# Reordering the head and the per-image table chain of a deformable convolution kernel

## The chip, the cores and the metric

The kernel runs on one core of one Trainium2 chip. Its time is the device time of one execution in microseconds (us), and the number quoted is the median of several runs. Engines are called by their names in the profile: PE is TensorE's matrix multiply (PEld its weight load), DVE is VectorE, ACT is ScalarE, POOL is GpSimd and SP is SyncE, which only issues DMAs. A name with a q behind it (SPq, ACTq, POOLq) is the queue of that engine, which issues DMAs in program order and waits for what they need.

## The reference

The input x is 8 images of 128 channels of 64 x 64 pixels, float32. There are two layers, each behind a group normalisation:

```
x = x + relu(batchnorm(deform_conv(groupnorm(x))))
x = x + expert_conv(groupnorm(x)) + shared_conv(groupnorm(x))
```

The change is in the first. Its deformable convolution first computes 27 maps of offsets and masks per image with a 3 x 3 convolution (`om`), and then, for each of 9 taps and each pixel, samples the image at a fractional place:

```
py = off_y + row + ky - 1;  px = off_x + column + kx - 1     # 9 taps
val = bilinear(x, py, px) * sigmoid(mask)
out = sum over channels and taps of val * w
```

The second layer mixes four expert kernels per image and convolves with the mixture.

## The kernel before

`dense()` is the first layer, `layer1()` the second. `general()` is a slow way for offsets of two pixels or more and does not run with these inputs.

**Bands.** An image is cut into 8 bands (`NB`) of 8 rows, and the main loop in `dense()` runs over 64 bands (and one closing turn). A band's bilinear sampling is done by matrix multiplication: for a row of 15 tiles (4 x 4 output pixels each, for two tile rows), the 8 x 8 surrounding pixels, turned by `pixels` (L630, ACT copies them out at L635), are multiplied in `sample` (L672) with weights `s`. `weights` (L656, VectorE) makes these as a product of two tents, `x_wts` and `y_wts`, three steps ahead. Then `conv` (L721) multiplies the samples with the taps' weights, in nine matmuls a band, called parts 0 to 8 below; the band after an image's last has 18.

**Tables.** The tents come from two tables per image in DRAM, `x_table` and `y_table`. `load_x` (L590) reads two rows of 576 KB each per band, three bands ahead, and `load_y` (L575) eight pieces of 90 KB per band, two bands ahead; in the main loop both go through POOL's queue. ACT (L606) and VectorE (L608) finish the x tents in `spread`.

**The table chain.** The tables of an image are made by the generator `tables(b)`, in this order: statistics of the image (L290), group means and deviations (L296 and L306 on PE, L312 on POOL), normalisation in place (L318 on ACT, L319 on VectorE), the offsets' convolution in four blocks (`combine` at L345 on VectorE, `tap` at L362 on PE), collecting in `om` (L385 to L395), a turned copy (L402 or L404/L405), stores to DRAM as `rowwise` (L408) and `colwise` (L412), loads back with rows and columns on partitions into `raw_off` (L435, L437), a nudge for the borders (L474), distances in y and x (L478, L487), the x table's store (L458), the mask (L523), five tents (L501, L505, or L510 to L516) times the mask (L537), and the y table's store (L527).

**The order is written out by hand.** Each `yield` in `tables(b)` gives back control, `pause(n)` gives it back n times, and `yield BLOCK` waits until a part in `BLOCKS`. The main loop takes some three steps (`tick`) at every part, so that the chain of a later image lies between the matmuls of an earlier one. Engines run in program order, so where a step is placed decides what queues behind it. The chain of image b + 2 begins in band 5 of image b, at part 4, and must be done one image later. Images 0 and 1 have a head: image 0's chain runs alone, and then image 1's as far as its group scale, before the first band.

The y table is stored skewed: the tent i of row h goes to row h + i of a table with 4 rows more, and the loads read along that diagonal.

Of the kernel before, what the change touches and what calls it, by code (L numbers as in the profile page):

```python
# [41 lines left out]
T = 4  # L42
# [22 lines left out]
def deform_moe_conv(  # L65
# [83 lines left out]
    def padded(pool, name):  # L149
# [12 lines left out]
        for a, n in (("y", (H + 2 * REACH) * GROW), ("x", NROW * XROW))  # L162
# [15 lines left out]
    def dense():  # L178

        with ExitStack() as st:  # L180
# [95 lines left out]

            def tables(b):

                if b == B:
                    return  # L280
                pad = pads[b % 2]
                stats = small.tile([P, NCH, 6], F32, name="stats")
                part = [
                    pad[:, ROWPAD + 8 * c : ROWPAD + 8 * c + 8].rearrange("p h w -> p (h w)")
                    for c in range(NCH)
                ]
                for c in range(NCH):
                    if c == 6 and b > 1:
                        yield from pause(14 if b > 2 else 24)
                    nc.vector.bn_stats(stats[:, c, :], part[c])  # L290
                    yield from pause(2)
                mv = small.tile([P, 2], F32, name="mv")
                nc.vector.bn_aggr(mv, stats)
# [23 lines left out]
                for c in range(0, NCH, 2):  # L317
                    nc.scalar.activation(part[c], part[c], AF.Identity, bias=shift, scale=scale)  # L318
                    nc.vector.tensor_scalar(  # L319
                        part[c + 1], part[c + 1], scale, shift, ALU.mult, ALU.add  # L320
                    )
                    yield from pause(2)
# [10 lines left out]
                def combine(j):  # L333
# [5 lines left out]
                    for half in range(2):  # L339
                        rows = [  # L340
                            pad[:, ROWPAD - 1 + H // 2 * half + i :][:, 0 : H // 2 : 2]
                            for i in (lo, hi)
                        ]
                        n = H // 4
                        nc.vector.tensor_tensor(  # L345
                            combo_of[j][:, half * n : half * n + n], *rows, op
                        )
                        yield from pause(2)
# [7 lines left out]
                def tap(j, kx):  # L356

                    if kx == 1:
                        pcs[j] = ps_c.tile([P, CH], F32, name="pc", tag="pc")
                    lo, hi = max(0, 1 - kx), min(W, W + 1 - kx)  # L360
# [26 lines left out]
                yield from block(2)  # L387
                m2 = taken(2)
                nc.vector.tensor_tensor(odd, even, m2, ALU.subtract)
                nc.vector.tensor_tensor(even, even, m2, ALU.add)  # L390
                yield from combine(3)
# [7 lines left out]
                if b:  # L399
                    for half in (slice(0, H // 8), slice(H // 8, H // 4)):  # L400
                        yield from pause(2)
                        nc.scalar.copy(turned[:, half], by_rows[:, half])  # L402
                else:
                    nc.scalar.copy(turned[:, 0 : H // 8], by_rows[:, 0 : H // 8])  # L404
                    nc.vector.tensor_copy(turned[:, H // 8 :], by_rows[:, H // 8 :])  # L405
                yield from pause(4)
                for j in range(4):
# [3 lines left out]
                    )  # L411
                    (nc.gpsimd if b or j % 2 == 0 else nc.sync).dma_start(  # L412
                        out=colwise[b][:, :, H // 4 * j : H // 4 * (j + 1)],
                        in_=omc[32 * j + 9 : 32 * j + 18],
                    )
                nc.vector.tensor_reduce(
                    most[:, b : b + 1], omr, AX.X, ALU.max, apply_absolute_value=True
                )
                if b == 0:
                    for g in range(2):  # L420
                        pick(g)
                yield from pause(12)
                by_row = rowwise[b].rearrange("h (t k u) w -> h t k (u w)", t=3, k=3)

                for k in range(3):
# [6 lines left out]
                    for outs, parts, v in places:  # L434
                        nc.sync.dma_start(out=raw_off[parts, v], in_=by_row[outs, 0::2, k])  # L435
                        parts = slice(W + parts.start, W + parts.stop)
                        (nc.gpsimd if b or k == 1 else nc.scalar).dma_start(  # L437
                            out=raw_off[parts, v, 0].rearrange("p (u h) -> p u h", u=3),
                            in_=colwise[b][k::3].rearrange("s w h -> w s h")[outs],
                        )  # L440
                if b == 0:
                    for _ in pixels(0):
                        pass
                yield from pause(26)
# [28 lines left out]
                for i in range(2):  # L473
                    nc.vector.tensor_scalar(  # L474
                        raw_off[:, 2 * i, 0], raw_off[:, 2 * i, 0], nudge[:, i : i + 1],
                        None, ALU.add,
                    )
                nc.vector.tensor_copy(by_y, moved(0, 0, "v", "j", "u"))  # L478
                nc.vector.tensor_copy(by_y[:, :, 0, 0], raw_off[sides[0], :, 0, 2 * W])
                nc.vector.tensor_copy(by_y[:, :, W - 1, 2], raw_off[sides[0], :, 0, W - 1])  # L480
                yield from pause(2)
                for out_, in_ in (
                    (by_x, moved(1, 0, "j", "u", "v")),
                    (by_x[:, 0, 0], raw_off[sides[1], :, 0, 2 * W]),
                    (by_x[:, W - 1, 2], raw_off[sides[1], :, 0, W - 1]),
                ):
                    nc.vector.tensor_scalar(out_, in_, in_tile, None, ALU.add)  # L487
                if b:
                    store_x(0, NROW // 2, nc.sync)
                    store_x(NROW // 2, NROW, nc.sync)  # L490
                else:
                    store_x(0, 2, nc.gpsimd)
                    store_x(2, 6, nc.sync)
                yield from pause(2)
# [921 lines left out]
```

## Time and profile before

| what | value |
|---|---|
| median of 3 runs | 1520.25 us (1520.05 to 1520.77) |
| the profiled execution | 1525.29 us, its span 1523.6 us |
| PE busy | 1362.8 us, 89% |
| DVE, ACT, POOL busy | 975.4, 831.0, 527.4 us |
| mean granted PE clock | 0.96 |
| moved by DMA | 227.34 MB, mean 149 GB/s |

The span is from the first to the last instruction. A line of the timeline has start, duration, engine, source line, operation, tile written and tile read, count, and in brackets the idle time before it and what ended it. Lines of waits have who waited for what: total us, times, and the longest.

### The profile page before, as it was taken

Reading aid. Unit: us, or ns where it says so; the run is one execution under the profiler, and the core shown is the slowest. Engines: PE = TensorE matmul, PEld = TensorE weight load, DVE = VectorE, ACT = ScalarE, POOL = GpSimd, SP = SyncE. Lnnn points to the kernel's source line nnn. Section 1 sums busy time; section 2 is a strip of 40 time slices with the busy share of each in tenths; the row PEclk is TensorE's granted clock in tenths of the full one; section 3 lists DMA queues with packets and bytes.
Section 4 is the critical chain, followed back from the end, with each engine's and each line's share of the span. In section 5 each row is a group of like instructions: output and inputs, shape, how many; then the busy total and the mean of one; then the engine's idle time right before and its main releaser. Section 6 shows DMA issues by size and latency. Waiting matters only on the chain. (4 is left out here: it accounts for less than half of the span.)

```text
span 1523.6 us, 21317 instructions
## 1 busy us (share of the span) xinstructions
PE 1362.8 (89%) x7714; PEld 761.6 (50%) x7714; DVE 975.4 (64%) x1905; ACT 831.0 (55%) x1124; POOL 527.4 (35%) x824
## 2 busy tenths in 40 slices
PE   3159899999999989998999999999993899999998
PEld 1044455555555555655555565566551344444443
DVE  5547565666656656655665665655428888889972
ACT  2245664776686567667657766866634333323320
POOL 2222432543353254334425434543303223332300
PEclk9579999999999999999999999999996899999999
DMA  3555884996787589678858967878707044444111
GB/s 129 133 128 113 185 177 105 175 217 133 138 201 173 123 155 221 126 136 199 170 126 168 214 137 142 183 171 200 165 26 302 30 164 166 166 152 166 51 46 58
DMA packets 113932, 227.34 MB, mean 149 GB/s; under 512 B 62238, under 2 KB 68670, under 8 KB 105625
## 3 DMA queue, kind: packets, MB, share of 16 engines
q0 software_dynamic: 52464, 123.79, 40.3%
q1 hardware_dynamic: 59703, 101.03, 21.2%
q8 instruction: 63, 1.03, 0.3%
q10 hardware_dynamic: 1650, 1.06, 0.2%
q14 instruction: 52, 0.43, 0.1%
HBM read 180.23 MB, written 45.35 MB: 148 GB/s over the span
## 5 line engine op out<-in xcount | busy, mean ns | idle before, releaser
L721 PE MATMUL py<-samples,dw_sb 128*128 128x512 f32 (+3 forms) x1296 | 580.1, 565 | 3.1 <-DVE samples L699 1.8
L575 POOL DMA_DIRECT2D ywts<-taby x496 | 294.1, 608 | 303.7 <-DMA xwts<-tabx 244.1
L672 PE MATMUL pq<-s,xt 64*128 64x144 f32 (+1 forms) x3840 | 279.4, 298 | 27.7 <-DVE s L656 19.6
L721 PEld LDWEIGHTS py<-samples,dw_sb 128*128 128x128 f32 x1296 | 219.3, 191 | 156.6 <-issue 134.5
L682 ACT COPY samples<-pq 128x864 f32<-128x864 f32 (+1 forms) x320 | 281.7, 977 | 26.2 <-PE pq L672 26.0
L672 PEld LDWEIGHTS pq<-s,xt 64*128 64x128 f32 x3840 | 253.8, 188 | 77.3 <-issue 30.0
L656 DVE TENSOR_TENSOR s<-xwts,ywts 128x432 f32<-128x432 f32 (+1 forms) x448 | 199.1, 497 | 134.7 <-DMA ywts<-taby 44.9
L635 ACT COPY xt<-pt 128x512 f32<-128x512 f32 (+1 forms) x256 | 142.2, 556 | 175.1 <-PE pt L630 164.7
L630 PEld LDWEIGHTS pt<-ident,picked 128*128 128x128 f32 x960 | 112.1, 142 | 185.0 <-ACT xt L635 116.1
L630 PE MATMUL pt<-ident,picked 128*128 128x128 f32 x960 | 154.1, 281 | 42.7 <-ACT xt L635 38.0
L608 DVE TENSOR_SCALAR xwts<-xwts 128x1152 f32<-128x1152 f32 (+2 forms) x130 | 97.5, 750 | 140.8 <-ACT xwts L606 140.4
L1328 PE MATMUL pc<-v,u 128*128 128x512 f32 x384 | 172.8, 599 | 9.3 <-DVE u L1276 9.3
L1328 PE MATMUL pc<-v,wmix 128*128 128x512 f32 x384 | 177.1, 606 | 0.0
L606 ACT ACTIVATE xwts<-xwts,place 128x1152 f32<-128x1152 f32 (+2 forms) x130 | 161.0, 1242 | 26.3 <-DMA ywts<-taby 20.3
L590 POOL DMA_DIRECT2D xwts<-tabx x128 | 73.2, 577 | 254.8 <-DVE s L656 242.2
L1306 ACT ACTIVATE t<-pc,bmix 128x512 f32<-128x512 f32 x32 | 22.0, 687 | 182.9 <-PE pc L1328 100.9
L1328 PEld LDWEIGHTS pc<-v,u 128*128 128x128 f32 x384 | 72.4, 190 | 98.3 <-issue 85.1
L1328 PEld LDWEIGHTS pc<-v,wmix 128*128 128x128 f32 x384 | 72.7, 192 | 88.9 <-issue 85.2
L729 ACT ACTIVATE y<-py,db_sb 128x512 f32<-128x512 f32 (+3 forms) x72 | 45.8, 636 | 90.8 <-PE py L721 52.3
L345 DVE TENSOR_TENSOR combo<-pad 128x1024 f32<-128x1024 f32 x64 | 75.2, 1220 | 21.8 <-PE pc L362 15.7
L615 DVE COPY picked<-pad 128x960 f32<-128x960 f32 x128 | 82.3, 683 | 0.0
L1155 POOL TENSOR_TENSOR x<-x,xt 128x512 f32<-128x512 f32 x32 | 45.8, 1464 | 85.7 <-ACT x L1153 85.7
(162 smaller groups left out, 1064.9 us busy)
## 6 DMA issues: line engine op xcount, KB each, us to landing
xwts<-tabx POOLq DMA_DIRECT2D x128, 576.0 KB, 7.8
ywts<-taby POOLq DMA_DIRECT2D x496, 90.0 KB, 8.3
pad<-in_x_dram SPq DMA_DIRECT2D x48, 512.0 KB
out_dram<-yo SPq DMA_DIRECT2D x32, 512.0 KB
yd<-y SPq DMA_DIRECT2D x48, 256.0 KB
pad<-yd SPq DMA_DIRECT2D x16, 512.0 KB
x<-yd SPq DMA_DIRECT2D x16, 512.0 KB
xt<-in_x_dram SPq DMA_DIRECT2D x16, 512.0 KB
```

Source lines behind the costliest of these rows:

```text
L345: nc.vector.tensor_tensor(combo_of[j][:, half * n : half * n + n], *rows, op)
L575: engine.dma_start(out=y_wts[g % 2][at : at + NR * Q, r].rearrange("p a b c -> p (a b c)"), in_=bass.AP(tensor=y_table[b].tensor, offset=y ...
L606: nc.scalar.activation(part, part, AF.Abs, bias=column)
L608: nc.vector.tensor_scalar(part, part, -1.0, 0.0, ALU.add, ALU.min)
L615: nc.vector.tensor_copy(picked[g % 2][:, :, h], bass.AP(tensor=one.tensor, offset=one.offset, ap=[list(one.ap[0]), [T, NCOL], [W, Q], [1, Q]],
L630: nc.tensor.transpose(pt[:, c], picked[g % 2][:, c0 + c].rearrange("p h y x -> p (h y x)"), ident,)
L635: nc.scalar.copy(xts[g][:, c0 : c0 + n], pt[:, 0:n])
L656: nc.vector.tensor_tensor(s[:, :, 3 * at : 3 * (at + k)].rearrange("p m (c x) -> p m c x", x=3), by_x[:, :, c : c + k], by_y[:, :, w : w + ...
L672: nc.tensor.matmul(by_m[:, h, :, at : at + k], lhsT=xts[g][rows, c], rhs=s[rows, :, at : at + k], start=True, stop=True,)
L682: nc.scalar.copy(bass.AP(tensor=one.tensor, offset=one.offset + first, ap=[list(one.ap[0]), [M * PLANE, 2], [PLANE, M], [WB + 1, 3], [1, w ...
L721: nc.tensor.matmul(py, lhsT=dw_sb[:, 3 * (2 - yy) + 2 - xx], rhs=samples[g % 2][:, m : m + 3 * n - 2 : 3, xx, 1 : W + 1], start=(i == 0), ...
L1328: nc.tensor.matmul(pc, lhsT=us[j][:, kx], rhs=vs[g][:, rows, kx : kx + W], start=(kx == 0), stop=(kx == 2),)
```

## The change

- `statistics(b)` becomes a generator of its own. In the main loop, its eight steps are taken one per part in bands 6 and 7 of the image two before; `tables(b)` starts at part 2 of band 7, where it was part 4 of band 5. What is left of the chain before is finished at the start of band 6, where it was part 4 of band 5.
- In the chain, the pause between the stores of `om` and their loads grows from 12 to 16 steps, that between the loads and the nudge from 26 to 34, and those around each tent shrink from 3 and 4 to 2 and 2. All rowwise stores now come before all colwise ones.
- The y table is plain: row h holds its five tents side by side.
- For image 0: normalisation has three parts on ACT and five on VectorE; the negation of the taps' weights (`dw_sb`, L766) goes behind the tables; upper halves of three of the four combinations go to GpSimd; the blocks take PSUM buffers of their own (`ps_q`); colwise loads go to SP and GpSimd, behind the rowwise ones; the y side of the nudge and distances no longer waits for the x side; the first y stores have 16 of the 64 rows, the rest comes last; the pixel copies, statistics of image 1, and the loads of later bands change places.

Cut to its core:

```diff
-        for a, n in (("y", (H + 2 * REACH) * GROW), ("x", NROW * XROW))
+        for a, n in (("y", H * GROW), ("x", NROW * XROW))
...
+            def statistics(b):
+                if b >= B:
+                    return
+                stats = small.tile([P, NCH, 6], F32, name="stats")
+                for c, part in enumerate(chunks(b)):
+                    nc.vector.bn_stats(stats[:, c, :], part)
+                    if c == NCH - 1:
+                        means[b] = small.tile([P, 2], F32, name="mv")
+                        nc.vector.bn_aggr(means[b], stats)
+                    yield
...
-                for c in range(NCH):
-                    if c == 6 and b > 1:
-                        yield from pause(14 if b > 2 else 24)
-                    nc.vector.bn_stats(stats[:, c, :], part[c])
-                    yield from pause(2)
-                mv = small.tile([P, 2], F32, name="mv")
-                nc.vector.bn_aggr(mv, stats)
+                mv = means.pop(b)
                 yield BLOCK
...
+                for c in range(NCH):
+                    if c in (0, 2, 4, 6) and (b or c < 6):
+                        nc.scalar.activation(part[c], part[c], AF.Identity, bias=shift, scale=scale)
+                    else:
+                        nc.vector.tensor_scalar(part[c], part[c], scale, shift, ALU.mult, ALU.add)
+                        yield from pause(2)
...
-                        nc.vector.tensor_tensor(
+                        (nc.vector if b or j == 1 or half == 0 else nc.gpsimd).tensor_tensor(
...
-                    if kx == 1:
+                    if kx == 1 and b:
                         pcs[j] = ps_c.tile([P, CH], F32, name="pc", tag="pc")
+                    elif kx == 1:
+                        pcs[j] = ps_q.tile([P, 2, CH], F32, name="pq")[:, 0]
...
-                yield from pause(12)
+                yield from pause(16)
...
+                        if b:
+                            turned_in(nc.gpsimd, k, outs, parts, v)
+                        else:
+                            by_column.append((k, outs, parts, v))
+                for k, *where in by_column:
+                    turned_in(nc.sync if k == 0 else nc.gpsimd, k, *where)
+                yield from pause(34)
-                if b == 0:
-                    for _ in pixels(0):
-                        pass
-                yield from pause(26)
...
-                            offset=y_table[b].offset + i * GROW + (NR - 1 - i) * YSTEP,
-                            ap=[[GROW, H], [GROW - YSTEP, n], [1, YSTEP]],
+                            offset=y_table[b].offset + rows.start * GROW + i * YSTEP,
+                            ap=[[GROW, rows.stop - rows.start], [1, n * YSTEP]],
...
                         yield from tent(i)
-                        yield from pause(3)
+                        yield from pause(2)
                         masked(i)
-                        yield from pause(4)
+                        yield from pause(2)
...
-                load_x(0, nc.gpsimd)
-                for i, k in ((0, 3), (1, 4), (2, None)):
-                    for _ in tent(i):
-                        pass
-                    masked(i)
-                    store_y(i, 1)
-                    if k:
-                        other_tent(k)
-                        masked(k)
-                        store_y(k, 1)
+                for i in (3, 4):
+                    other_tent(i)
+                nudged(sides[1])
+                distances_x()
+                store_x(0, 2, nc.gpsimd)
+                load_x(0, nc.gpsimd)
+                for i in (0, 1, 2):
+                    for _ in tent(i):
+                        pass
+                soon = slice(0, 4 * T)
+                for i in (3, 0, 4, 1, 2):
+                    masked(i)
+                    store_y(i, 1, soon)
+                for _ in pixels(0):
+                    pass
+                for k in range(2 * T):
+                    load_y(0, k, nc.scalar if k in (1, 4, 7) else nc.sync)
+                for _ in statistics(1):
+                    pass
                 for slots in ((NCOL * T, XROW // XSTEP), (0, 12), (12, 36), (36, NCOL * T)):
                     spread(0, slots)
-                for k in range(2 * T):
-                    load_y(0, k, nc.scalar if k % 2 else nc.sync)
-                for g in (1, 2):
-                    load_x(g, nc.gpsimd)
+                store_x(2, 6, nc.gpsimd)
+                load_x(1, nc.gpsimd)
+                for k in range(2 * T):
+                    load_y(1, k, nc.sync)
+                load_x(2, nc.gpsimd)
                 store_x(6, NROW, nc.gpsimd)
-                for k in range(2 * T):
-                    load_y(1, k, nc.scalar if k < 4 else nc.sync)
+                store_y(0, NR, slice(4 * T, H))
...
+                if j == NB - 2:
+                    for _ in made:
+                        pass
+                    asked, made, means_of = True, iter(()), statistics(b + 2)
...
+                    if odd == 0 and (j == NB - 2 and part < 6 or j == NB - 1 and part < 2):
+                        next(means_of, None)
+                    if odd == 0 and j == NB - 1 and part == 2 and b + 2 < B:
+                        made = tables(b + 2)
+                        next(made)
...
-                        if j == 5:
-                            for _ in made:
-                                pass
-                            asked = False
-                            made = tables(b + 2) if b + 2 < B else iter(())
```

## The prediction

> **What bounds the kernel now.** The sum is made on the profiled execution: span 1523.6 us, 1525.29 us in all. The median of the other runs is 1520.25 us, 5.0 us below; I carry differences over to it unchanged. 0.2% (3.0 us) is about what a measurement of this kernel can tell from no change.
>
> First the page's second part, 40 slices of 38.1 us.
>
> ```profile
> PE   3159899999999989998999999999993899999998
> ...
> PEclk9579999999999999999999999999996899999999
> ```
>
> TensorE is full in the bands; only the first two or three slices (the head) and slice 31 (into the second layer, not touched) are empty. So a shift of the head counts in full, and in the bands only idle TensorE time counts. Next the timeline of the head.
>
> ```profile
> 59.89 6.64 SPq L527 DMA_DIRECT2D taby<-work  x5
> 59.96 2.66 POOL L590 DMA_DIRECT2D xwts<-tabx  x5
> ...
> 79.02 11.63 ACTq L575 DMA_DIRECT2D ywts<-taby  x8
> 79.05 10.20 SPq L575 DMA_DIRECT2D ywts<-taby  x8
> 90.86 1.80 DVE L656 TENSOR_TENSOR s<-xwts,ywts 128x432 f32<-128x432 f32 x4 [12.61 <-DMA ywts<-taby]
> ```
>
> The five y stores are issued by 66.5 and the first y load starts at 79.02: 12.5 us of landing. The loads take 11.8 us more. The stretches (PE, PEld, DVE, ACT, POOL busy, then clock, DMA share, GB/s) say why:
>
> ```profile
> 66.00:72.00 6.00, 0.00 (x0) 0.00 (x0) 2.78 (x7) 2.77 (x4) 0.00 (x0) 0.50 1.02 257
> 72.00:78.00 6.00, 1.08 (x4) 1.00 (x4) 4.68 (x11) 0.00 (x0) 0.00 (x0) 0.50 1.00 258
> 84.00:90.00 6.00, 0.00 (x0) 0.00 (x0) 0.00 (x0) 0.00 (x0) 0.00 (x0) 0.50 0.30 109
> ```
>
> Until 78 the DMA engines are full: six x loads of 576 KB (3.46 MB) and 0.74 MB of y stores. While only y loads run they move 109 GB/s at a share of 0.30. Last, TensorE's waits from 120 to 1125:
>
> ```profile
> PE pt L630 <- ACT xt L635: 25.8, 8, 6.7
> PE pq L672 <- ACT samples L682: 7.8, 8, 1.3
> ```
>
> By image, the first is 6.7, 1.0 (1.3 with one of 0.3), 3.0, 5.9, 4.7, 3.4, 0.7 for images 1 to 7. Image 4's, in the timelines of VectorE and ScalarE:
>
> ```profile
> 559.37 1.79 DVE L656 TENSOR_TENSOR s<-xwts,ywts 128x432 f32<-128x432 f32 x4 [9.12 <-DMA combo<-colwise]
> 561.08 0.54 DVE L474 TENSOR_SCALAR combo<-combo,nudge 128x192 f32<-128x192 f32 x2
> ...
> 561.65 1.20 ACT L523 ACTIVATE combo<-combo 64x576 f32<-64x576 f32 x3 [5.55 <-DVE combo L474]
> ...
> 564.19 0.56 ACT L635 COPY xt<-pt 128x512 f32<-128x512 f32 x1
> ```
>
> VectorE waits for late y loads, the nudge (L474) queues behind, ScalarE waits at the mask (L523), and the copy that TensorE needs is behind the mask.
>
> **Head, up to the offsets.** The ScalarE negation of dw (L766, ended 19.4) goes behind; its normalisation can start at 14.0 like VectorE's: 3 x 0.73 = 2.2 there, 5 x 0.48 = 2.4 on VectorE, done 16.4. The first combination started at 20.89: -4.4. The next three blocks' upper halves go to GpSimd. No 1024-element one is in the trace; 128x528 took 1.10, 128x512 mean 1.46 and at most 2.36 (L1155), so 2.1 to 4.7, and I take 2.9, twice the mean beside a busy VectorE. The Trainium skill (GPSIMD Engine Reference, Key points) speaks against this: GpSimd shares its SBUF interfaces with VectorE instructions that have two SBUF inputs, as the halves beside it have; the 2.36 may be that, and at 4.7 the next sum loses 2 us. With own PSUM buffers, blocks 2, 0 and 3 follow block 1 (17.7 + 5.05 = 22.8) at 2.8 to 2.9 each: 31.3, last subtraction 0.7, offsets at 32.1 instead of 39.6: **-7.5** (-5 at 4.7).
>
> **Head, offsets to y stores.** Rowwise stores go ahead of all colwise ones. Before, the last was issued by 42.46 and its loads began at 47.58, 5.1 later with colwise pieces ahead; a colwise load of 48 KB landed in 2.3. Between these I take 3.3, so SP's loads of them start 1.2 + 3.3 = 4.5 us after the offsets instead of 8.0; SP's two colwise stores (0.84 + 2.22) end before that. Five issues 2.9 and 1.8 landing: nudge of the y side at +9.2, 41.3 (before, for both sides, 52.85). From there VectorE's queue decides: nudge 0.55, distances 1.1, two other tents 2 x 1.65, second nudge 0.55, x distances 1.1, five masks 3.7: 51.7. ScalarE's mask and three tents (1.2 + 4.3) lie beside it, since the pixel copies now follow. The x side has slack of 1.3 at the second nudge (46.3): its stores landed at +9.4 and are issued 0.8 sooner, and GpSimd's three loads take 3 x 0.66 and 2.3, so 45.0; later than that costs directly. Before, the last mask ended 66.05: **-14.3** in all, of which 7.5 were the offsets.
>
> **Head, y stores and loads.** The first y stores carry 16 of 64 rows, 37 KB each; x loads of bands 1 and 2 come behind. Landing was 12.5; 48 KB landed in 2.3, the x load of one band alone is 1.15 MB / 258 GB/s = 4.5. So 2.3 to 6.8; I take 4: last issue 52.2, loads from 56.2, **-22.8**. Eight loads are needed; alone, half of the 17.4 us that 16 took (79.05 to 96.44, when VectorE stopped waiting for the second eight) is 8.7. But x loads of bands 1 and 2, 2.3 MB or 9 us at 258 GB/s, now run beside them instead of under the stores: at most 8.7 + 9 = 17.7, or 11.8 + 9 = 20.8 by the old time. I take 15.5, nearer the upper ends since x shares filled the engines in the rows above: first sum at 71.7 instead of 90.86, **-19** (-11 to -25.5, from both landings and both loads). The Trainium skill (DMA: Bandwidth & Descriptors, Queues, rings and completion order) is harsher: engines take turns between queues by whole packets. If x packets then move four bytes to one of y, all 9 us fall on y and the sum would be -14. Under the y wait lie: image 1's statistics (5.2 on VectorE); the x stores (issue 48.1), the x load 3.6 later and 8.3 to land as before, 60.0, and its spread (3.3) to 63.3; the chain's steps to L309 (2.0) to 65.3; on ScalarE's queue the pixel copies (47 to 54), three y loads (0.71 each) and the negation (1.16). If y loads came at once, 65.3 would be the first sum. Behind: band 2's loads wait for the other 48 rows, stored after 13 y loads on SP; VectorE asks for them 14 us after the first sum and TensorE 30 us after it (L672 at 122.49 against 91.67), so nothing to 3 us; I take 0.
>
> **Plain y table.** Same bytes and load shape (40 pieces of 2304 B). The steady store has 64 pieces of 11.5 KB instead of 320. It is issued a band before its loads, which cover its landing. No row shows another row distance; TensorE's waits for L656 are 4.3 us in all, which could go or double. I take 0 (-4 to +4).
>
> **Bands.** Counting the hand-written steps through the band loop: statistics go one per part into bands 6 and 7, the chain starts in band 7, and in images 3 to 7 the colwise stores come in band 2 part 1 (before band 1 part 6), the loads in part 6, the nudge in band 4 part 0 (before band 3 part 1). GpSimd's queue carries both and the next x and y loads. Before's image 1 shows the new order: stores after a band's y loads.
>
> ```profile
> 159.41 3.61 POOL L412 DMA_DIRECT2D colwise<-om  x4 [0.52 <-issue]
> 169.46 3.25 POOL L437 DMA_DIRECT2D combo<-colwise  x5 [6.44 <-DMA colwise<-om]
> 172.70 1.06 POOL L590 DMA_DIRECT2D xwts<-tabx  x2
> 173.75 3.46 POOL L575 DMA_DIRECT2D ywts<-taby  x6
> ```
>
> The band that began at 160.6 gets its x load at 172.7, 12.1 into it, and the last y load lands at 187.96 (VectorE waited until then), 13.4 into the next 14-us band. That next band is where the new nudge stands, so the late y loads block it again, a band later. In image 4 VectorE came free 559.37 - 546.95 (that band's first L672) = 12.4 into its band and TensorE lost 5.9, that is 6.5 less. The chain is tighter now (pause 2, not 3 and 4), one more tent (1.45) stands ahead of the copy: loss = free - 5.0. From below: no late load, 0; from above image 1's 13.4: 8.4. Nearest are the same images now, whose times of coming free, by that rule from their losses, are 9.5, 12.4, 11.2, 9.9, 7.2: losses 4.5, 7.4, 6.2, 4.9, 2.2 = 25.2 against 17.7. Image 1's nudge comes 3 parts later: 6.7 to about 4.5. Image 2's 5 parts later: 1.3 to 0. Sum 29.7 against 25.7: **+4**. The normalisation moves one part, leaving three instead of four 0.8-us steps ahead of the samples' copy: of the 1.0 lost there about 0.8 in 6 images goes, -4. Its own new wait: the group sum (L296) stands one part (1.1 us) behind the last statistics on VectorE, with TensorE's queue behind it: L656 waited 31.1 us for y loads in 14 bands, 2.2 each; 6 images at 0 to 2, I take 0.5: +3. Bands: **+3** (-26, all stalls gone, to +30).
>
> **Sum:** -19 + 3 = -16: 1504 us.
>
> **Rivals.**
> - Pauses do their work: colwise stores drain between two bands' loads, frees stay below 5, stalls of 25.7 fall to 5: -21 instead of +4, bands -22, so 1479; with half of that, 1490. For: the gap from loads to nudge grows from 26 to 34 steps. Against: image 1 in this order is late. 0.14.
> - The head gives back: y loads at 20.8 (-13.8) and band 2 late by 3, so -10.8, and the bands' +3: 1512. For: full DMA engines until 78. Against: y loads were underway 3 us before. 0.12.
> - **Slower:** the nudge behind late y loads. Image 1's 13.4 in images 3 to 7: 5 x 8.4 = 42 + 4.5, +20.8; the group sum's waits at 2.2 in 6 images +13; normalisation 0: +34, with -19 the result is 1535; with half of the waits, 1528. It decides once the bands lose over 19. For: full queue on GpSimd. Against: image 7, without loads of x, lost only 0.7. 0.14.
> - The likeliest, 1504; with the head between -12 and -24 and the bands as summed, 1499 to 1511. 0.60.
>
> Range 1486 to 1523: half of the first rival and the slower one lie outside, 0.2. Faster by over 0.2%: 0.60 + 0.14 + nearly all of the head's rival, less the bands' odds of +16: 0.81; within 0.06; slower 0.13.
>
> **What would show it.** First L656 at 70 to 74 (at 77 the loads' upper end, at 65 no contention); offsets stored near 32; y loads from 56. In the bands, waits of TensorE for xt copies of 22 to 35 us, with mask waits in band 4 of an image: near zero is the first rival, over 45 the slower one; a wait of TensorE's L296 for mv over 1 us an image is my new wait. I am wrong if the first L656 stays above 80, or if colwise stores in their new place delay the x loads by less than 5 us.

## The result and the profile after

The changed kernel takes 1531.80 us (median of 4 runs, 1530.70 to 1531.94), the kernel before beside it 1520.15 us (4 runs, 1519.23 to 1520.77): a ratio of 1.0076, 95% interval 1.0058 to 1.0093, so +11.65 us. Forecast were 1504 us, and 1486 to 1523. The profiled execution after took 1531.87 us (span 1529.8). That of before lay 5.1 us above its median and this one does not, so the two traces differ by 6.6 us only, and what follows accounts for those.

The timeline of VectorE after, at the end of the offsets, at the first y-side nudge and at the first sum of bands 0 and 1 (start, duration, line, operation, tiles, count, idle time and what ended it):

```profile
31.54 0.69 DVE L415 TENSOR_TENSOR om<-om,pq 128x512 f32<-128x512 f32 x1 [2.64 <-PE pq L379]
...
42.94 0.54 DVE L506 TENSOR_SCALAR combo<-combo,nudge 64x192 f32<-64x192 f32 x2 [6.44 <-DMA combo<-rowwise]
...
71.16 1.79 DVE L705 TENSOR_TENSOR s<-xwts,ywts 128x432 f32<-128x432 f32 x4 [4.00 <-DMA ywts<-taby]
...
88.24 1.79 DVE L705 TENSOR_TENSOR s<-xwts,ywts 128x432 f32<-128x432 f32 x4 [5.87 <-DMA taby<-work]
```

The offsets end 7.4 us sooner and the first sum starts at 71.16 instead of 90.86, 19.7 sooner. But band 1's first sum waits until 88.24, for its y loads: the last row names the y table's last store, which shares a semaphore with one of these loads, but by the trace's semaphore records the last of them landed at 87.76, and in kernels 5, 8 and 12 below the sum also starts 0.48 us after the last of them. Band 0's first output (the activation of y on ScalarE) is written at 110.31 instead of 122.60: the gain is 12.3 there, 15.4 in band 6 of image 0, 7.4 in band 6 of image 3, and from band 3 of image 6 on the kernel is 7.1 us late. The six intervals of an image with a table chain beside it (band 6 to the next image's band 6) went from 132.3, 131.6, 134.5, 132.9, 131.7, 125.8 to 133.8, 136.3, 136.4, 136.3, 136.5, 132.0; the one without is 111.7 in both.

TensorE's waits after, from 110 to 1137, the bands (waiting line, what it waited for, us in all, times, longest); before, from 122 to 1130, the same lines had 25.8, 7.8, 0.7 and 4.3:

```profile
PE pt L679 <- ACT xt L684: 32.8, 6, 6.8
PE pq L721 <- ACT samples L731: 11.5, 8, 5.2
PE py L770 <- ACT y L778: 4.7, 7, 0.7
PE pq L721 <- DVE s L705: 4.2, 2, 3.8
```

All waits together grew from 41.1 to 54.6, by 13.5, and TensorE's busy time for the same matmuls by 6.2 (965.29 to 971.49 in these windows). That is 19.7, which carries the 19.4 lost between the first output and the last. The mean clock of the two windows is 0.98 after and 0.99 before: it is low behind a long wait. Stretches around the wait of image 3 (PE, PEld, DVE, ACT, POOL busy, then clock, DMA share, GB/s):

```profile
424.00:430.00 6.00, 4.23 (x13) 1.70 (x11) 1.79 (x5) 1.28 (x2) 3.42 (x6) 1.00 0.87 207
430.00:436.00 6.00, 1.00 (x4) 1.01 (x5) 5.61 (x14) 5.41 (x9) 2.79 (x5) 0.78 1.02 178
436.00:442.00 6.00, 6.00 (x40) 3.42 (x41) 4.31 (x8) 5.58 (x10) 0.11 (x1) 0.66 0.85 175
```

The wait ends at 435.0; in stretches of 2 us the clock is 0.50 from 434 to 440, then 0.97 and 1.00.

Where that wait comes from, in the timelines of GpSimd, VectorE and TensorE; the band's first sampling matmul began at 402.26:

```profile
401.82 3.15 POOL L432 DMA_DIRECT2D colwise<-om  x4 [1.32 <-ACT xt L684]
411.81 3.39 POOL L452 DMA_DIRECT2D combo<-colwise  x5 [6.85 <-DMA colwise<-om]
415.20 1.34 POOL L639 DMA_DIRECT2D xwts<-tabx  x2
416.52 3.73 POOL L624 DMA_DIRECT2D ywts<-taby  x6
```

```profile
428.21 1.79 DVE L705 TENSOR_TENSOR s<-xwts,ywts 128x432 f32<-128x432 f32 x4 [8.64 <-DMA ywts<-taby]
429.92 0.55 DVE L506 TENSOR_SCALAR combo<-combo,nudge 128x192 f32<-128x192 f32 x2
```

```profile
435.00 0.90 PE L679 MATMUL pt<-ident,picked 128*128 128x128 f32 x3 [6.77 <-ACT xt L684]
```

The column-wise loads wait 6.85 us on GpSimd's queue for their stores to land, the x loads that the band issues for a later one stand behind them and go out 12.9 us into the band, the y loads behind those; VectorE waits for them, the nudge is queued behind the sums, and TensorE loses 6.8 us at the copy of xt. The Trainium skill (Perfetto Trace Analysis, Tensor Engine Instruction) says that GpSimd, VectorE and ScalarE work strictly in order; these rows agree, since the x loads leave as the 3.39 us of the column-wise loads end.

The same late nudge costs TensorE two waits under other names. In image 1 the nudge waits for the column-wise loads, ScalarE's mask and tents follow it, and the samples' copies stand behind them (VectorE, ScalarE and TensorE):

```profile
162.16 0.55 DVE L506 TENSOR_SCALAR combo<-combo,nudge 128x192 f32<-128x192 f32 x2 [4.14 <-DMA combo<-colwise]
162.74 1.20 ACT L562 ACTIVATE combo<-combo 64x576 f32<-64x576 f32 x3 [1.57 <-DVE combo L506]
170.11 3.49 PE L721 MATMUL pq<-s,xt 64*128 64x144 f32 x24 [5.21 <-ACT samples L731]
```

In image 2 the sums queue on VectorE behind late loads and the nudge, and TensorE waits 3.83 us for them at 288.99. With these two the nudge costs 32.8 + 5.2 + 3.8 = 41.8 us, against 25.8 before.

The waits for y have another cause. Before, in an image's last band, a block of the chain's matmuls stood between the two groups of its output, so that TensorE did not see the copy of the first; after, the block stands elsewhere (TensorE before, then after):

```profile
370.98 2.76 PE L362 MATMUL pc<-combo,offu_sb 128*32 128x512 f32 x24
```

```profile
357.84 1.15 PE L770 MATMUL py<-samples,dw_sb 128*128 128x256 f32 x4 [0.67 <-ACT y L778]
```

### The profile page after: what moved, and what is told of

It is laid out like the page before. It is cut to its first block, busy times and chain, and to the rows that moved or that the text cites. A ratio compares the mean times of both kernels' runs of the same rounds, so it can differ in the third digit from the quotient of the medians.

```text
span 1529.8 us, 21363 instructions
## 1 busy us (share of the span) xinstructions
PE 1371.9 (90%) x7714; PEld 769.0 (50%) x7714; DVE 974.3 (64%) x1905; ACT 828.7 (54%) x1123; POOL 544.5 (36%) x832
## 4 chain that ended last, share of the span: by engine, by line
PE 67%; DMA 13%; ACT 7%; DVE 4%; POOL 4%; issue 3%; SPq 1%; DVEq 0%; POOLq 0%; ACTq 0%
PE py L770 23%; PE pc L1383 21%; PE pq L721 12%; DMA xwts<-tabx 7%; PE pt L679 5%; PE pc L379 5%; DMA colwise<-om 2%; ACT xwts L655 2%; POOL combo L452 2%; ACT xt L684 1%; DMA ywts<-taby 1%; POOL colwise L432 1%; ACT pad L332 1%; ACT work L540 1%; ACT work L544 1%
## 5 line engine op out<-in xcount | busy, mean ns | idle before, releaser
L721 PE MATMUL pq<-s,xt 64*128 64x144 f32 (+1 forms) x3840 | 285.2, 303 | 26.6 <-DVE s L705 15.0
L721 PEld LDWEIGHTS pq<-s,xt 64*128 64x128 f32 x3840 | 259.4, 191 | 77.4 <-DVE xwts L657 29.2
L679 PE MATMUL pt<-ident,picked 128*128 128x128 f32 x960 | 155.0, 282 | 54.3 <-ACT xt L684 51.7
```

The source lines that it names most:

```text
L679: nc.tensor.transpose(pt[:, c], picked[g % 2][:, c0 + c].rearrange("p h y x -> p (h y x)"), ident,)
L721: nc.tensor.matmul(by_m[:, h, :, at : at + k], lhsT=xts[g][rows, c], rhs=s[rows, :, at : at + k], start=True, stop=True,)
```

## The experiments

Theory at the start: the head brings what its rows say, and the bands lose it at this queue. Rivals: the plain y table, the place of the statistics, and the DMA engines themselves. Several groups of runs were made, each with runs of the kernel before beside it (medians 1522.1 to 1523.1). Kernels of different groups are compared by their ratios; the last column gives a ratio as a difference from 1520.15 us.

| kernel | median, us | ratio to before, 95% interval | difference, us |
|---|---|---|---|
| after | 1531.80 | 1.0076 [1.0058, 1.0093] | +11.6 |
| 1 old bands, rest as after | 1510.32 | 0.9922 [0.9905, 0.9939] | -11.9 |
| 2 before, with the new bands | 1544.49 | 1.0147 [1.0117, 1.0177] | +22.3 |
| 3 after, column-wise transfers on SyncE | 1529.05 | 1.0041 [1.0019, 1.0064] | +6.2 |
| 4 after, later nudge | 1528.11 | 1.0050 [1.0031, 1.0070] | +7.6 |
| 5 as 1, band 1's spread later | 1508.91 | 0.9912 [0.9879, 0.9946] | -13.4 |
| 6 3 and 4 together | 1519.61 | 0.9974 [0.9953, 0.9995] | -4.0 |
| 7 as 1, later nudge | 1511.72 | 0.9920 [0.9894, 0.9947] | -12.2 |
| 8 as 5, x of band 2 behind y of band 1 | 1514.35 | 0.9947 [0.9927, 0.9967] | -8.1 |
| 9 after, no column-wise table | 1506.64 | 0.9900 [0.9874, 0.9926] | -15.2 |
| 10 as 1, no column-wise table | 1493.88 | 0.9816 [0.9792, 0.9840] | -28.0 |
| 11 after, x loads ahead of column-wise loads | 1516.89 | 0.9957 [0.9939, 0.9975] | -6.5 |
| 12 as 8, y table's other rows first | 1513.19 | 0.9919 [0.9894, 0.9945] | -12.3 |

**1. Old bands with the new head and the plain table.** The statistics go back into the chain (for images 2 on), the chain starts in band 5 again, and the old pauses return.

```diff
+                if b > 1:
+                    stats = small.tile([P, NCH, 6], F32, name="stats")
...
-                yield from pause(16)
+                yield from pause(12)
...
-                yield from pause(34)
+                yield from pause(26)
...
-                    asked, made, means_of = True, iter(()), statistics(b + 2)
...
-                        next(means_of, None)
...
+                        if j == 5:
...
+                            made = tables(b + 2) if b + 2 < B else iter(())
```

> The changed head and the plain y table, with the chain in the bands as before: statistics inside it from band 5 on, pauses 12, 26, 3 and 4. My theory: the head is worth 12 us at the second band (the offset of the y activations of the two traces), and all that is lost is lost in the bands, since y loads behind the colwise transfers in GpSimd's queue hold VectorE, the nudge and ScalarE's mask in one band. Then 1520 - 12 = 1508 (1504 to 1513), with waits of TensorE for xt copies near the 25 us of before. Rival, the plain table slows every y load: the loss is spread over the bands and stays, 1520 or more.

**2. The new bands alone**, on the kernel before, with its head and its skewed table: the same edits the other way.

```diff
-                yield from pause(12)
+                yield from pause(16)
...
-                yield from pause(26)
+                yield from pause(34)
...
+                    asked, made, means_of = True, iter(()), statistics(b + 2)
...
-                        if j == 5:
...
-                            made = tables(b + 2) if b + 2 < B else iter(())
```

> The kernel before, with only the chain's new places: statistics in bands 6 and 7, start in band 7, pauses 16, 34, 2 and 2. Head and skewed y table as before. My theory: the bands lose as much as in the changed kernel, 20 to 24 us: 1542 (1537 to 1547), and TensorE waits over 30 us for xt copies. Rival, plain table: 1520 to 1530.

Measured -11.9 and +22.3 us. Their sum, +10.4, is the change's +11.6 within the intervals, so head (with the plain table) and bands add up. The table itself can be told from the traces, from the first output to the last: 1038.2 us after and 1039.0 with the new bands and the skewed table, 1015.6 with the old bands and the plain table and 1018.8 before. So the plain table costs nothing that these runs can tell. TensorE's waits for xt in images 3 to 7 sum to 31.9 us after and 31.0 with the new bands alone, against 17.7 before.

**3. The column-wise stores and loads on SyncE.**

```diff
-                    (nc.gpsimd if b or j % 2 == 0 else nc.sync).dma_start(
+                    (nc.sync if b or j % 2 else nc.gpsimd).dma_start(
                         out=colwise[b]...
-                            turned_in(nc.gpsimd, k, outs, parts, v)
+                            turned_in(nc.sync, k, outs, parts, v)
```

> The changed kernel with the colwise stores and loads of images 1 to 7 in SP's queue instead of GpSimd's. My theory: GpSimd issues each band's x loads 1 to 3 us into it, the y loads come in time, and the xt waits of images 3 to 7 (32 us and a slow clock behind them) shrink to under 8: 1531.8 - 30 = 1502 (1495 to 1508). Rival, the small colwise pieces fill the DMA engines whichever queue issues them: y loads stay late, 1525 or more.

It gave 5.4 us of the 30 expected; its profiled execution lay 4.5 us above its median. The x loads left at 410.37 and 424.37, but SyncE took 8.73 us to issue the stores, and its queue had not issued the last column-wise load until 427.8. The wait changed its name only, in VectorE's timeline of this kernel:

```profile
429.20 1.81 DVE L705 TENSOR_TENSOR s<-xwts,ywts 128x432 f32<-128x432 f32 x4 [3.69 <-DMA xwts<-tabx]
435.42 0.55 DVE L506 TENSOR_SCALAR combo<-combo,nudge 128x192 f32<-128x192 f32 x2 [4.40 <-DMA combo<-colwise]
```

**4. A later nudge** in images 3 to 7, so that VectorE does not come to it with late sums ahead.

```diff
-                yield from pause(34)
+                yield from pause(58 if b > 2 else 34)
```

> The changed kernel with the pause before the nudge 58 instead of 34 in images 3 to 7: nudge and x distances at the end of band 4, mask and tents in band 5. Colwise transfers and their lateness stay. My theory: y loads still come late and VectorE still waits some 10 us in band 4, but no copy that TensorE needs is behind the mask, so the xt waits of these images fall from 32 to under 8: 1531.8 - 28 = 1504 (1498 to 1512). Rival, late y loads starve TensorE wherever the nudge is: 1526 or more.

It gave 4.0 us of the 28 expected. The waits did leave the xt copy, and most came back at the sums and the samples' copies (TensorE's waits of this kernel, 70 to 1130, in an execution 7.7 us below its median; after, in the same window, 15.0, 11.5 and 36.0):

```profile
PE pq L721 <- DVE s L705: 22.7, 9, 5.2
PE pq L721 <- ACT samples L731: 19.1, 15, 4.6
PE pt L679 <- ACT xt L684: 13.1, 10, 1.9
```

**6. Both together.**

```diff
-                    (nc.gpsimd if b or j % 2 == 0 else nc.sync).dma_start(
+                    (nc.sync if b or j % 2 else nc.gpsimd).dma_start(
                         out=colwise[b]...
-                            turned_in(nc.gpsimd, k, outs, parts, v)
+                            turned_in(nc.sync, k, outs, parts, v)
-                yield from pause(34)
+                yield from pause(58 if b > 2 else 34)
```

> The changed kernel with the colwise transfers of images 1 to 7 on SP's queue (as in e3) and the pause before the nudge 58 in images 3 to 7 (as in e4). In e3 the x loads were in time, but the nudge waited for the colwise loads themselves, which SP issued by 427.8 and which landed at 435.4; in e4 the late y loads remained. My theory: with both, neither VectorE's y loads nor the nudge are late in images 3 to 7, and TensorE's waits in each fall from some 9 us to under 3: 1531.8 - 30 = 1502 (1496 to 1511). Rival, the transfers slow one another on the DMA engines whichever queue and place: 1518 or more.

15.6 us better than after by the ratios, so the two edits together do more than either, but about half of the 30 expected. In its profiled execution, 9.3 us above its median, the second and third interval fell to 132.8 and 132.2 us; the two behind them were 135.5 and 136.7, with samples and sums waited for.

**7. The later nudge with the old bands.**

```diff
-                yield from pause(26)
+                yield from pause(47 if b > 2 else 26)
```

> The kernel of e1 (new head, old bands) with the pause before the nudge 47 instead of 26 in images 3 to 7: the nudge moves from band 3 part 1 to its part 8, out from behind the late y loads and ahead of them in nothing. My theory: the xt waits of images 3 to 7 (13.0 us in e1's trace) go, and as e4 showed, about half comes back as waits for sums and samples: 1510.3 - 7 = 1503 (1500 to 1507). Rival, all of it comes back: 1510 (1508 to 1512).

The rival was right: -12.2 beside -11.9. From 70 to 1130, the waits for xt fell from 25.9 in kernel 1 to 14.7, and those for sums rose from 13.9 to 30.4. Here a late sum costs TensorE as much as the late nudge did.

**9 and 10. No column-wise table** in images 3 to 7, with the new and with the old bands.

```diff
-                for j in range(4):
+                for j in range(4 if b < 3 else 0):
                     ...  out=colwise[b]
...
-                        if b:
+                        if b > 2:
+                            pass
+                        elif b:
                             turned_in(nc.gpsimd, k, outs, parts, v)
```

> The kernel after, with the column-wise stores and loads of images 3 to 7 left out, so that the x-side offsets of these images are stale. Theory (the loss in the bands comes from this table's way through DRAM: what waits for it on GpSimd, and the time it takes from the x and y loads): the interval of a band goes from 136.4 to 126 to 128 us and the time to 1490 to 1497 us. Rival (the place of the statistics, or the y and x loads by themselves, carry it): 1520 us or more.

> The new head and the plain table with the old bands, and the same stores and loads left out, so that the x-side offsets of images 3 to 7 are stale. Theory: the old bands lose their smaller waits as well, 1485 to 1492 us, and the two kernels without the column-wise table are within 5 us of each other: the whole loss is where these transfers stand. Rival (the place of the statistics counts too): the kernel after without them stays 10 us or more above this one.

Kernel 9 lies between its two cases: an image's interval (which its expectation calls a band's) is 130.2 to 131.3 in the middle of the run. In 10 the rival holds: the kernels without the table stay 12.8 us apart. Without these transfers the new bands lose 26.8 us of their time and the old ones 16.1; so their cost is 10.7 us more in the new place. TensorE's waits of the new bands without the table (110 to 1111), and then of the old bands without it (110 to 1099):

```profile
PE pq L723 <- ACT samples L733: 23.0, 13, 5.2
PE pt L681 <- ACT xt L686: 7.5, 6, 1.3
PE py L772 <- ACT y L780: 4.7, 7, 0.7
```

```profile
PE pq L733 <- ACT samples L743: 12.6, 12, 2.5
PE pt L691 <- ACT xt L696: 8.0, 3, 6.1
...
PE py L782 <- ACT y L790: 0.7, 1, 0.7
```

The sums for xt are alike now, but the old bands have theirs in images 1 and 2, the new ones in images 3 to 7. What remains stands at the samples (+10.4) and at y (+4.0, the block that stands elsewhere); TensorE's busy time is 2.7 more, its waits for sums 3.6 less. In images 3 to 7 the nudge is no longer late, and what is left is ScalarE's mask and tents, which stand ahead of the last xt copies and the samples' copies; TensorE's rows in image 3, with the new and then with the old bands:

```profile
431.11 0.55 PE L681 MATMUL pt<-ident,picked 128*128 128x128 f32 x3 [1.32 <-ACT xt L686]
437.56 1.93 PE L723 MATMUL pq<-s,xt 64*128 64x144 f32 x24 [1.62 <-ACT samples L733]
```

```profile
420.73 1.92 PE L733 MATMUL pq<-s,xt 64*128 64x144 f32 x24 [0.81 <-ACT samples L743]
```

These rows fit the tighter pauses around the tents (2 and 2, not 3 and 4); no run changed the pauses alone.

**11. The x loads ahead of the column-wise loads**, on the same queue; no instruction is added or left out.

```diff
-                        if b:
-                            turned_in(nc.gpsimd, k, outs, parts, v)
-                        else:
-                            by_column.append((k, outs, parts, v))
+                        by_column.append((k, outs, parts, v))
+                if b > 1:
+                    yield from pause(8)
                 for k, *where in by_column:
-                    turned_in(nc.sync if k == 0 else nc.gpsimd, k, *where)
-                yield from pause(34)
+                    turned_in(nc.sync if b == 0 and k == 0 else nc.gpsimd, k, *where)
+                yield from pause(34 - (8 if b > 1 else 0))
```

> The kernel after, with the five column-wise loads of images 2 to 7 issued 8 ticks later, so that on GpSimd the next band's two x loads and eight y loads stand between the column-wise stores and the loads that wait for them; the pause up to the nudge is shorter by as much, and the other engines' orders are the same. Theory (the x loads are late because they stand behind a wait on their queue: 6.85 us for the column-wise stores to land, then 3.39 us for the loads): in image 3 the x loads go out near 404 us instead of 415.2, the waits of 6.8 us per image fall to 2 us or less, the interval of a band comes near the 130.3 us of the kernel without the column-wise table, and the time to about 1504 us (1500 to 1510). Rival (the transfers themselves take the time, and a wait that is moved comes back elsewhere, as with the late nudge): waits for sums, samples or the nudge take their place and the time stays at 1524 us or more.

18.1 us less than after by the ratios (14.9 by the medians): about two thirds of what the theory asked, and the most of any full kernel with the new bands, though its interval touches that of 6. Its profiled execution lay 3.4 us above its median. GpSimd's timeline of this kernel:

```profile
404.99 3.14 POOL L432 DMA_DIRECT2D colwise<-om  x4 [1.21 <-ACT xt L684]
408.12 1.28 POOL L639 DMA_DIRECT2D xwts<-tabx  x2
409.38 1.78 POOL L624 DMA_DIRECT2D ywts<-taby  x3
...
422.79 1.95 POOL L452 DMA_DIRECT2D combo<-colwise  x3 [0.85 <-PE pq L721]
425.02 1.31 POOL L452 DMA_DIRECT2D combo<-colwise  x2 [0.29 <-DMA ywts<-taby]
426.33 1.06 POOL L639 DMA_DIRECT2D xwts<-tabx  x2
```

The x loads go out as soon as the stores are issued, at 408.12 instead of 415.20, although the band begins 3 us later here. The column-wise loads now start at 422.79, and the next band's x loads stand behind them. The waits for xt in images 3 to 7 fell from 31.9 to 18.0 (2.7, 3.3, 3.9, 5.1, 3.0), and the clock of 430 to 440 us rose from 0.67 to 1.00; the waits for samples rose from 11.5 to 17.6 (5.1 of it in image 2, where after had waited 3.8 for the sums).

**5, 8 and 12. The head's give-back.** After, ScalarE's spread of band 1's x tents waits for x loads until 78.00 (the chain of waits has their landing from 64.45 on), VectorE's half of it stands ahead of band 0's last sums, and TensorE idles 5.86 us until 81.85. In 5 it is issued behind them; in 8 also the x loads of band 2, and the x store after them, go behind band 1's y loads; 12 moves a y store ahead of these.

```diff
-            for slots in HALVES:            # 5: out of the head
-                spread(1, slots)
...
+                    if g == 0 and q == 2:   # 5: into band 0
+                        for slots in HALVES:
+                            spread(1, slots)
...
-                load_x(2, nc.gpsimd)
-                store_x(6, NROW, nc.gpsimd)
+                store_y(0, NR, slice(4 * T, H))   # 12 only: ahead of these
+                load_x(2, nc.sync)                # 8 and 12
+                store_x(6, NROW, nc.sync)
-                store_y(0, NR, slice(4 * T, H))   # 12 only
```

> The kernel of e1 (new head, old bands) with one move: the spread of band 1's x weights comes after the first band's first two sampling steps instead of before them. In the changed kernel's trace the first sum is at 71.2, but TensorE then stands 5.9 us for the sums of steps 3 and 4, which queue on VectorE behind that spread, whose x loads landed at 78.0. My theory: the head's 19.7 us at the first sum shrink to 12.3 at the second band by this queueing: 1510.3 - 5 = 1505 (1503 to 1507.5). Rival, the DMA engines are full there, and what is won waits for band 1's loads instead: 1510 (1509 to 1511.5).

> The new head, the plain table and the old bands with spread(1) after the third step of band 0, and besides the x loads of band 2 and the second store of the first x table issued on SyncE, so behind the y loads of band 1. Theory (the y loads of band 1 land late, at 88.24 us, because other transfers share the 16 DMA engines with them): without these two beside them they land at 84 us or sooner and the time is about 1505 us (1502 to 1507). Rival (the y loads are bound by their own rate and by the order in which SyncE issues them): they land at 88 us again and the time stays at 1509.

> As the kernel with the x loads of band 2 behind the y loads of band 1, with the store of the y table's remaining rows on SyncE put ahead of these x loads and of the store that follows them. Theory (moving the x transfers away did bring band 1's y loads forward by 4.1 us, and the time was lost because the remaining rows, and with them band 2's y loads, stood behind the x loads): the first sum of band 1 stays near 84 us, the first of band 2 comes back to 99 us or sooner, and the time falls to about 1505 us (1503 to 1508). Rival (the same bytes must cross in the same time, so what band 1 gains band 2 loses): band 2's first sum stays past 101 us and the time at 1509 us or more.

The 5.86 went away in 5, where TensorE runs the 60 matmuls of band 0 through without a gap, yet band 1's matmuls start at 89.05 instead of 90.60, since its first sum is at 88.24 as in the kernel after. So 5 gained 1.5 us on 1 of the 5 expected, which the intervals do not tell from nothing, and its rival's reason holds. In 8 band 1's first sum came at 84.15, so the theory was right on contention, but the time was 5.3 us above 5 (the intervals overlap): band 2's first sum came at 103.19 instead of 98.73. In 12 it came at 101.67; the rival holds, though 12 is not told from 5 by its interval. VectorE's timeline of kernel 12, the first sums of bands 0, 1 and 2:

```profile
70.03 2.31 DVE L715 TENSOR_TENSOR s<-xwts,ywts 128x432 f32<-128x432 f32 x5 [3.50 <-DMA ywts<-taby]
...
83.56 1.79 DVE L715 TENSOR_TENSOR s<-xwts,ywts 128x432 f32<-128x432 f32 x4 [4.16 <-DMA xwts<-tabx]
...
101.67 1.79 DVE L715 TENSOR_TENSOR s<-xwts,ywts 128x432 f32<-128x432 f32 x4 [8.77 <-DMA ywts<-taby]
```

What one band gains the next one loses here. The fastest full kernels are those with the old bands: 5 has 0.9912 of the kernel before, and 1, 7 and 12 are not told from it.

## Why the prediction was wrong, point by point

Two terms of the sum failed: what stands behind the first sum, taken at 0, cost 7.4 us, and the bands, taken at +3, cost 19.4.

- **Head up to the first sum: right in time, partly by luck.** Offsets predicted at 32.1, measured 32.2, though the first block's matmuls began at 19.30 where I had 17.7; last mask 51.7 and 53.2, 1.5 late since SyncE's five rowwise loads took 4.35 us (37.01 to 41.36) to issue, where I had 2.9; y loads from 56.2 and 55.05; first sum 71.7 and 71.16. The stores' landing, taken at 4 with 2.3 as the least, was 1.5 (53.57 to 55.05), which made up for the late mask. With four bytes of x moved to one of y, the prediction's own reading of the turns by whole packets in the Trainium skill (DMA: Bandwidth & Descriptors, Queues, rings and completion order), the first sum would have been near 77. It was not; but the x loads of band 1 went out at 63.91 only, when all y loads of band 0 had been issued, so this run tests the page's turns in part.
- **Head, behind the first sum: wrong.** "Nothing to 3 us; I take 0" was the step that failed: it looked at band 2's rows only, and band 1's x and y loads, at 78.0 and 88.24, were later than the first sum allowed. It cost 7.4 us in the traces. The rival "the head gives back" had -10.8 for the head; -11.9 was measured in kernel 1. It had the first sum late, which it was not; its cause, full transfers, is supported by 8 and 12.
- **Bands, waits of the nudge: right in mechanism, 12 us too small.** Predicted 29.7 in all (25.2 in images 3 to 7, 4.5 in image 1, 0 in image 2), measured 41.8 (31.9, 5.2 and 4.7), of which 32.8 at the xt copies. The mechanism, the late x loads behind the column-wise wait, was the one predicted, to 0.8 us (12.1 and 12.9 into the band), and 11, which takes them out of it, won 18.1 us by the ratios. But images 3 to 7 all lose 5.2 to 6.8, near image 1's old 6.7; I took losses of 2.2 to 7.4 from these images' old times of coming free, where the order had become image 1's. And I counted the waits at the xt copies alone, where images 1 and 2 wait at the samples and the sums.
- **Bands, clock: left out.** Behind a wait of 6.8 us the clock was 0.66 for 6 us; busy time grew 6.2.
- **Bands, normalisation: wrong.** Predicted -4. Three steps do stand ahead of the samples' copy instead of four, but the wait there in images 3 to 7 only went from 1.0 to 0.9 each.
- **Bands, waits for y: left out.** A wait of 0.7 stands in the last bands of seven images instead of one, +4.0, since the count did not ask which waits a moved block had hidden.
- **Bands, the group sum's own wait: wrong, harmless.** Predicted +3; the waits for mv before (1.6) went, and none came.
- **Plain table: right,** 0 within what the traces of 1 and 2 tell.
- **Sum.** In the traces the head gives -12.3 where -19 stood, the bands +19.4 where +3 stood. The slower rival's place (0.14) was nearer than my sum. It took image 1's order for every image, which is what happened, at 5.2 to 6.8 us an image where it had 8.4. Its +34 for the bands was 15 too much and its head 7 too good, so that its 1535 came near 1531.8 is partly luck. I had spread the chance by single mechanisms, though this one and the head's rival share a cause, the transfers, and came together.

Two things stay open. The 12.8 us that remain between the bands without the column-wise table were read from rows; no run tried the pauses around the tents or the moved block apart. And 11 still lies 5.4 us above 1 by the ratios; whether an order with the column-wise loads between x and y loads would close that was not tried.

## What to carry to other kernels

An instruction that waits on a DMA queue delays everything issued behind it, so when a step is moved, read what the queue issues next at the new place (here x loads; putting them first won 18.1 us by the ratios), and take the price from the row that already has that order, not from the same step's old rows. Moving a wait to a later point can merely rename it, as in 4 and 7 here; check by summing all waits of the bounding engine and its busy time, since its clock can be low behind a long wait. A head that is shortened up to its first result must be followed until the second and third results, which need transfers that the first did not. And ask of every block that is moved which wait it had hidden at its old place.

## What the runs showed of the hardware

GpSimd's timeline after, the upper halves of the three combinations:

```profile
16.54 5.50 POOL L360 TENSOR_TENSOR combo<-pad 128x1024 f32<-128x1024 f32 x1 [2.73 <-DVE pad L336]
22.33 6.35 POOL L360 TENSOR_TENSOR combo<-pad 128x1024 f32<-128x1024 f32 x2 [0.29 <-PE pq L379]
```

The first took 5.50 us beside three of VectorE's (3.49 in all), above my upper bound of 4.7; the other two took 3.2 each, with VectorE in such combinations for some 3 of these 6.35 us; one of VectorE's own took 2.17 beside them, where its median is 1.22. The Trainium skill's note on the shared SBUF interfaces (GPSIMD Engine Reference, Key points) would fit this, but no run separates it from other causes. The offsets ended as predicted all the same.

Four stores of the column-wise table went out in 3.15 us but held the loads behind them until 10 us after the first was issued; on SyncE's queue issuing the same four took 8.73 us.
